# VectorE of layer 0's attention in written order, with row work and routing in parts

## The chip, the cores and the metric

One Trainium2 chip, of which the kernel uses one core. The core has TensorE (PE, matmuls into PSUM banks), VectorE (DVE), ScalarE (ACT), GpSimd (POOL) and SyncE (SP, whose queue issues most DMAs); each works through its own list of instructions in a fixed order, and semaphores make one wait for another. The metric is the device time of one execution in microseconds.

## The reference

Two layers over x of 8 x 512 x 512 (batch, row, feature), float32. Layer 0 is causal attention with 16 heads of 32, then a mixture of 8 experts of which each row uses two; after each a layer norm. Layer 1 (attention with 8 query heads over 2 key heads, then a quantised FFN) is not touched by the change. Layer 0, cut to what matters:

```python
q, k, v = (x @ W.T + b for W, b in ((WQ_w, WQ_b), (WK_w, WK_b), (WV_w, WV_b)))      # in heads
attn = softmax(where(causal, -inf, q @ k.T / sqrt(32)))
x = layernorm(x + (attn @ v) @ WO_w.T + WO_b)
probs = softmax(x @ gate_weight.T + x @ (2.0 * gate_lora_B @ gate_lora_A).T)
routing_weights, selected = top_k(probs, 2)          # and divided by their sum
x = layernorm(x + sum over the two of weight * expert(x))
```

## The kernel before

Attention of layer 0 (`attention0`, lines 1353 to 1823) runs over 8 batches b. A batch has 4 groups g of 4 heads, and a group has 3 units u, which are the key tiles (0), (1, 3) and (2) of the causal triangle. One pass of the innermost loop is called the slot (g,u) here: 12 slots a batch. A slot issues, in the order of its text:

- `scores` (L1603): matmuls of q and k into the one room `sc` (four PSUM banks), for the third unit of batches 1 to 6 preceded by `deltas` (adapters of the experts); ScalarE's exp to `p`, GpSimd's `affine_select` of the causal diagonal, and beside them other GpSimd work: `watch_inverses` (adds r_inv to g_total, L1129), the addition of the bias row to x (L1638; for batch 0 in one instruction, L1641), and the merging of adapters into expert weights (L874);
- `todo[g, u]`: work planned for this slot, mostly matmuls with the addition that takes their result out of the bank;
- `waiting` (`product`, L1647): p times values of the slot before into `av`, and VectorE's sums of p of the units over the keys (`total`, L1665, for the second and third unit);
- `late[g, u]`: more planned work;
- in the second unit `summing` (`normalise`, L1668) of the group before: matmuls `rs` of `total` with ones; ScalarE's copy, Ln and Exp; VectorE's two steps that refine the inverse (L80, L81), and the product with av into aoT (L1679).

`plan` (L1692) says what lies in which slot. Query, key and value matrices of batches 1 to 7 are made by a scheme with seven products instead of eight (`queries_and_keys`, `values`; their matmuls `ps_1of7` to `ps_7of7` in the order 1, 6, 2, 5, 3, 7, 4). The sums of blocks that feed them are `seven_of_weights` (once, L812) and `seven_of_rows` (per batch, on xT, L825). `project` (L1528) multiplies aoT by wo, adds it to x, and after the fourth row tile calls `env.layernorm` (L217 to L225: statistics, then GpSimd's rstd, then four normed row tiles, each stored to DRAM). `blocks` (L1556) transposes the normed rows in 32 x 32 blocks on VectorE and sends them through DRAM to get x transposed; `score` (L1575) makes router logits of it, `choose` (L1587, L537) the two experts of each row in some 26 small VectorE instructions, `dispatch` (L1590) the rank of each row in its expert in 13, `one_hot` and `enter` (L1595, L1600) put rows into the table of tiles.

Results of matmuls other than sc, av and (before) ps_r lie in two banks that alternate, `mm`. A matmul into one of them waits until the content from two calls back has been read.

What sets the order: `in_order` (L70) fixes TensorE's list to the order of the text. VectorE, ScalarE, GpSimd and SP are not fixed in this part: a planner puts their instructions in an order by when it reckons them ready, at build time, and on the chip that order stands. `issue_after` (`behind_return`, L1550) makes instructions follow a given one on the same queue.

## Time and profile before

| | us |
|---|---|
| median of 3 runs | 2144.84 (2137.78 to 2147.74) |
| profiled execution | 2130.51, its span 2128.7 |
| granted TensorE clock | 0.996 |
| attention of layer 0, first scores to the last slot | 14.25 to 716.5 |
| one batch in the middle (batch 4) | 369.89 to 456.45 |
| TensorE busy in 197 to 628 (431 us, batches 2 to 6) | 397.91 |
| VectorE busy there | 325.21 |
| GpSimd busy there | 189.59 |

Start times below are microseconds from the start of the span. A timeline line is: start, length, engine, line of the kernel, operation, names of what it writes and reads, shapes, how many were merged into the line, and in brackets the idle time of the engine before it with what ended it. In the list of waits, `PE rs L1672 <- DVE qk L1472` reads: TensorE's matmul into rs waited for VectorE's instruction of line 1472. Seven-product matmuls have line 67, as all matmuls that go through the helper `matmul_by_columns`.

### The profile page before, as it was taken

The numbers are of one execution on the slowest core, as the hardware profiler recorded it, in microseconds if no ns is written. First come the engines' busy times: TensorE is split into PE (matmuls) and PEld (weight loads), VectorE is DVE, ScalarE is ACT, GpSimd is POOL, SyncE is SP. The second block draws the span as 40 slices with busy tenths as digits, with TensorE's granted clock in tenths as the row PEclk, the third lists the DMA queues.
The fourth block names the chain that finished last, engine by engine and source line by source line (L and its number), as shares of the span: only waits on it lengthen the run. The fifth ranks groups of instructions, "written<-read, shape, count | busy, mean of one in ns | idle before, by whom it ended". The sixth has DMA issues, their size and how long they took to land. (4 is left out here: it accounts for less than half of the span.)

```text
span 2128.7 us, 40459 instructions
## 1 busy us (share of the span) xinstructions
PE 2049.1 (96%) x17122; PEld 1117.1 (52%) x17122; DVE 1314.0 (62%) x2155; ACT 638.9 (30%) x930; POOL 517.3 (24%) x509
## 2 busy tenths in 40 slices
PE   8888999999997999999999999999999999999998
PEld 2334444444443677775433333333334888888886
DVE  4657876877867733224236888888857644555443
ACT  2334334343443211111133333333332232222222
POOL 1343534444443311132033312322201000000000
PEclk9999999999999999999999999999999999999999
DMA  6014425235154467887631322232201311111000
GB/s 204 2 57 124 141 80 144 88 103 155 61 176 169 169 169 222 248 243 214 188 113 51 114 75 72 98 119 75 65 1 47 102 60 60 60 60 60 20 20 22
DMA packets 193071, 226.29 MB, mean 106 GB/s; under 512 B 73818, under 2 KB 139610, under 8 KB 189298
## 3 DMA queue, kind: packets, MB, share of 16 engines
q1 hardware_dynamic: 180240, 185.44, 27.8%
q0 software_dynamic: 10560, 34.61, 5.6%
q10 hardware_dynamic: 2082, 3.56, 0.6%
q8 instruction: 138, 2.26, 0.4%
q14 instruction: 51, 0.42, 0.1%
HBM read 138.88 MB, written 84.69 MB: 105 GB/s over the span
## 5 line engine op out<-in xcount | busy, mean ns | idle before, releaser
L1618 ACT ACTIVATE p<-sc 128x2048 f32<-128x2048 f32 (+1 forms) x96 | 152.4, 1587 | 194.6 <-PE sc L67 194.6
L1628 POOL TENSOR_SCALAR_AFFINE_SELECT p<-p 128x512 f32<-128x512 f32 x128 | 98.4, 780 | 383.6 <-ACT p L1618 379.9
L1281 DVE SCALAR_TENSOR_TENSOR hT<-ps_u,vec,sg 128x512 f32<-128x512 f32 x88 | 65.5, 745 | 189.8 <-PE ps_u L1276 189.6
L1292 PE MATMUL ps_f<-ffn_w,h_half 128*128 128x512 f32 x664 | 167.6, 393 | 2.8 <-DVE h_half L1287 2.0
L1009 PE MATMUL ps_gu<-xrT,experts 128*128 128x256 f32 x736 | 166.7, 379 | 0.0
L1009 PEld LDWEIGHTS ps_gu<-xrT,experts 128*128 128x128 f32 x736 | 139.3, 190 | 35.9 <-issue 19.3
L1129 POOL TENSOR_TENSOR g_total<-g_total,r_inv 128x512 f32<-128x512 f32 x64 | 87.7, 1370 | 289.7 <-DVE r_inv L2035 270.6
L2005 ACT ACTIVATE p<-sc 128x1024 f32<-128x1024 f32 x128 | 124.2, 1022 | 100.0 <-PE sc L67 96.5
L1665 DVE TENSOR_TENSOR p<-p 128x1536 f32<-128x1536 f32 (+2 forms) x96 | 147.2, 1533 | 7.9 <-POOL p L1628 2.9
L2035 DVE RECIPROCAL r_inv<-r_inv 128x512 f32<-128x512 f32 x32 | 107.1, 3347 | 71.5 <-ACT r_inv L1126 71.5
L1292 PEld LDWEIGHTS ps_f<-ffn_w,h_half 128*128 128x128 f32 x664 | 122.9, 188 | 34.4 <-DVE h_half L1287 7.4
L1276 PE MATMUL ps_g<-x_high,ffn_w 128*128 128x512 f32 x352 | 137.2, 390 | 0.0
L1276 PE MATMUL ps_g<-x_low,ffn_w 128*128 128x512 f32 x352 | 137.0, 389 | 0.0
L1276 PE MATMUL ps_u<-x_low,ffn_w 128*128 128x512 f32 x352 | 136.9, 389 | 0.0
L1276 PE MATMUL ps_u<-x_high,ffn_w 128*128 128x512 f32 x352 | 136.9, 389 | 0.0
L67 PE MATMUL sc<-qT,kT 64*64 64x512 f32 x1024 | 124.7, 602 | 1.2 <-ACT qT L1899 0.9
L2024 PE MATMUL av<-p,v 128*64 128x512 f32 x512 | 120.8, 593 | 0.0
L1279 ACT ACTIVATE sg<-ps_g,vec 128x512 f32<-128x512 f32 x88 | 60.6, 688 | 195.4 <-PE ps_g L1276 195.4
L67 PE MATMUL ps_o<-attn_out,aoT 128*64 128x512 f32 x512 | 116.4, 598 | 0.0
L67 PE MATMUL ps_q<-hT,attn_qkv 128*64 128x512 f32 (+1 forms) x504 | 116.2, 596 | 0.0
L1126 ACT ACTIVATE r_inv<-rs 128x512 f32<-128x512 f32 x64 | 38.2, 597 | 254.6 <-PE rs L1672 109.2
L219 POOL TENSOR_SCALAR rstd<-mv 128x4 f32<-128x4 f32 x15 | 3.9, 260 | 452.9 <-DVE mv L218 452.9
(317 smaller groups left out, 3584.3 us busy)
## 6 DMA issues: line engine op xcount, KB each, us to landing
results<-y SPq DMA_DIRECT2D x68, 256.0 KB, 2.7
pair<-xrT SPq DMA_DIRECT2D x30, 512.0 KB, 3.1
xrT<-pair SPq DMA_DIRECT2D x120, 128.0 KB, 3.8
turned<-turned SPq DMA_DIRECT2D x56, 256.0 KB, 4.0
merged<-merged SPq DMA_DIRECT2D x48, 256.0 KB, 2.8
experts<-merged SPq DMA_DIRECT2D x8, 1536.0 KB, 8.3
x<-in_x SPq DMA_DIRECT2D x8, 1024.0 KB, 8.7
merged<-in_gate_up SPq DMA_DIRECT2D x32, 256.0 KB, 3.0
```

The source lines that it names most:

```text
L67: nc.tensor.matmul(out[m], lhsT=lhsT[:, m], rhs=rhs, start=start, stop=stop)
L1009: nc.tensor.matmul(ps[:, j, :], lhsT=w, rhs=xT[:, c, :], start=c == 0, stop=c == ND - 1)
L1129: self.nc.gpsimd.tensor_tensor(self.total, self.total, r_inv, ALU.add)
L1276: nc.tensor.matmul(ps, lhsT=w[:, ts(dc, P)], rhs=x[:, dc, :], start=(dc, i) == (0, 0), stop=(dc, i) == (ND - 1, 1))
L1281: nc.vector.scalar_tensor_tensor(hT, u, vec[:, V_SU + c : V_SU + c + 1], sg, ALU.mult, ALU.mult)
L1292: self.nc.tensor.matmul(os[t], lhsT=h[:, ts(t, P)], rhs=self.weights(2 * NHID + c), start=(c, i) == (0, 0), stop=(c, i) == (NHID - 1, 1))
L1618: nc.scalar.activation(p, sc[:, :, :width], AF.Exp, scale=scale)
L1628: select = nc.gpsimd.affine_select(out=first, in_=first, pattern=[[0, 4], [1, P]], compare_op=ALU.is_ge, fill=0.0, base=0, channel_multipl ...
L1665: nc.vector.tensor_tensor(total[:, :, P * kt :], total[:, :, P * kt :], p[:, :, at : at + w], ALU.add)
L2005: nc.scalar.activation(p, sc, AF.Exp, scale=scale)
L2024: nc.tensor.matmul(st["av"][HD * j : HD * (j + 1), :], lhsT=st["v"][:, kt, HD * j : HD * (j + 1)], rhs=p[:, j, :], start=kt == 0, stop=kt ...
L2035: nc.vector.reciprocal(r_inv, r_inv)
```

## The change

VectorE's list is fixed to the order of the text too, from the first query up to the slot (2,1) of the last batch; and the text is put in a new order.

- A slot now ends with `summed` (the sums of p of the slot before, split off `product`) and a third list, `after`.
- `normalise` ends with ScalarE's rough inverse; VectorE's part (`finish`) comes in the third unit of the slot after, behind `todo`.
- `project` takes its statistics with each row tile; `norm_rows` norms and stores two row tiles in `after` of (2,0) and two in (2,1). `blocks` is split over `after` of (2,2) and (3,0); the next x is loaded behind it.
- The router's logits move from (3,2) to (0,0) of the next batch, the matmul and first two steps of the choice to (0,1), its other 24 instructions (`pick`) to `after` of (0,1), the dispatch to `after` of (0,2), `one_hot` in halves to (1,0) and (1,1). ps_r lies in an mm bank and no longer in an av bank.
- Sums of blocks of weights and rows are split and spread; `spread` is made a slot ahead of its matmuls.
- In the last batch the products of the second pair of heads are spread from (0,0) to (2,2), and experts 1 and 2 are loaded a group later. `watch_inverses` moves from the third unit to the first.

```diff
-        nc.scalar.activation(tmp, tmp, AF.Exp)
+        nc.scalar.activation(tmp, tmp, AF.Exp)
+        return lambda: self.pick(here, pr, tmp, top, second, red, total, bc)
...
+            if t == 0:
+                stats[:] = env.small.tile([P, NT, 6], F32, name="stats"), env.small.tile([P, NT, 2], F32, name="mv")
+            nc.vector.bn_stats(out=stats[0][:, t, :], in_=xs[b][:, t, :])
+            nc.vector.bn_aggr(out=stats[1][:, t, :], in_=stats[0][:, t, :])
...
+        def norm_rows(b, *tiles):
+            for t in tiles:
+                x = xs[b][:, t, :]
+                nc.vector.tensor_scalar(x, x, stats[1][:, t, 0:1], stats[2][:, t : t + 1], ALU.subtract, ALU.mult)
+                nc.sync.dma_start(out=router.rows[router.row_at(b, t) :][:P], in_=x)
...
-            if u == 2 and inverses:
+            if u == 0 and inverses:
...
+        def sum_up(u, p, acc):
+            total, at = acc[0], 0
+            for kt in UNITS[u] if u else ():
                 w = S - P * kt
-                if u:
-                    nc.vector.tensor_tensor(total[:, :, P * kt :], total[:, :, P * kt :], p[:, :, at : at + w], ALU.add)
+                nc.vector.tensor_tensor(total[:, :, P * kt :], total[:, :, P * kt :], p[:, :, at : at + w], ALU.add)
...
-                inverse(nc, r_inv, rs, work.tile([P, S], F32, tag="r_inv", name="r_rough", bufs=2))
+                rough = rough_inverse(nc, rs, work.tile([P, S], F32, tag="r_inv", name="r_rough", bufs=2))
+            def finish():
+                if (b, g) != (NB - 1, ND - 1):
+                    inverse(nc, r_inv, rough)
+                normed[0] = nc.vector.tensor_tensor(aoTs[b][:, g, :], av, r_inv, ALU.mult)
...
                     (0, 0): [lambda: value(0, 0), lambda: value(0, 1)],
-                    (0, 1): [lambda: value(0, 3), lambda: query(0, 1)],
-                    (0, 2): [lambda: value(0, 2), lambda: key(0, 1), lambda: pair_of_heads(0, 1)],
-                    (1, 0): [lambda: router.merge_lora(mm([P, ND, E], "ps_wr")), lambda: query(0, 2), lambda: key(0, 2), x_sums],
-                    (1, 1): [lambda: query(0, 3), v_sums],
-                    (1, 2): [lambda: key(0, 3), q_sums, out_of_bias],
-                    (2, 0): [k_sums],
+                    (0, 1): [lambda: value(0, 3), lambda: query(0, 1), lambda: v_sums(False)],
+                    (0, 2): [lambda: value(0, 2), lambda: key(0, 1), lambda: pair_of_heads(0, 1), lambda: q_sums(False)],
+                    (1, 0): [lambda: router.merge_lora(mm([P, ND, E], "ps_wr")), lambda: query(0, 2), lambda: key(0, 2),
+                             lambda: v_sums(True), lambda: k_sums(False)],
+                    (1, 1): [lambda: query(0, 3), lambda: x_sums(False), spread_bias],
+                    (1, 2): [lambda: key(0, 3), out_of_bias, lambda: q_sums(True), lambda: x_sums(True)],
+                    (2, 0): [lambda: k_sums(True)],
...
-                    todo[2, 0].append(x_sums)
+                    late[1, 2].append(lambda: x_sums(False))
+                    late[2, 0].append(lambda: x_sums(True))
...
+                after[3, 0].append(lambda: load_next_x(b + 1))
             if b > 1:
-                todo[0, 0].append(lambda: choose(b - 2, mm=aside))
-                late[0, 2].append(lambda: dispatch(b - 2))
+                late[0, 0].append(lambda: score(b - 2))
+                todo[0, 1].append(lambda: picks.append(choose(b - 2)))
+                after[0, 1].append(lambda: picks[0]())
+                (late if last else after)[0, 2].append(lambda: dispatch(b - 2))
+                for places, slot in zip(((0, 1), (2, 3)), (((0, 2), (1, 0)) if last else ((1, 0), (1, 1)))):
+                    after[slot].append(lambda places=places: rows.append(one_hot(b - 2, places)))
+                todo[1, 2].append(lambda: enter(rows[-1]))
...
+                for tiles_of, slot in zip(((0, 1), (2, 3)), ((1, 1), (1, 2)) if last else ((2, 0), (2, 1))):
+                    after[slot].append(lambda tiles_of=tiles_of: norm_rows(pb, *tiles_of))
                 if by_dma:
-                    todo[2, 1].append(lambda: blocks(pb))
-                    late[3, 2].append(lambda: score(pb))
+                    after[2, 2].append(lambda: blocks(pb, 0, 1))
+                    after[3, 0].insert(0, lambda: blocks(pb, 2, 3))
...
-        order.enter_context(in_order(tc))
+        order.enter_context(in_order(tc, mybir.EngineType.DVE))
...
-                    for e in ((0,), (), (1, 2), (3, 4, 7))[g]:
+                    for e in ((0,), (), (), (1, 2, 3, 4, 7))[g]:
                         experts.load(e)
                 acc = []
                 for u in range(len(UNITS)):
                     p = scores(b, g, u)
                     for thunk in todo[g, u]:
                         thunk()
+                    if u == 2 and finish is not None:
+                        finish()
                     if waiting is not None:
                         waiting()
                     for thunk in late[g, u]:
                         thunk()
                     if u == 1 and summing is not None:
-                        summing()
+                        finish = summing()
+                    if summed is not None:
+                        summed()
+                    for thunk in after[g, u]:
+                        thunk()
                     waiting = lambda b=b, g=g, u=u, p=p, acc=acc: product(b, g, u, p, acc)
+                    summed = lambda u=u, p=p, acc=acc: sum_up(u, p, acc)
+                    if (b, g, u) == (NB - 1, 2, 1):
+                        order.close()
+                        order.enter_context(in_order(tc))
```

## The prediction

> **What bounds the kernel now.** First the page: TensorE (PE) is busy for 96% of the span, VectorE (DVE) for 62%.
>
> ```profile
> span 2128.7 us, 40459 instructions
> PE 2049.1 (96%) x17122; PEld 1117.1 (52%) x17122; DVE 1314.0 (62%) x2155; ACT 638.9 (30%) x930; POOL 517.3 (24%) x509
> ```
>
> So an edit of VectorE's order pays or costs only where TensorE stands still for VectorE. The list of waits, filtered to TensorE and to batches 2 to 6 (197 to 628 us), shows where; the columns are total, times, longest:
>
> ```profile
> PE rs L1672 <- DVE qk L1472: 10.5, 10, 1.1
> PE ps_4of L67 <- DVE experts L1472: 6.9, 5, 1.4
> PE ps_3of L67 <- DVE qk L1472: 4.7, 5, 0.9
> PE ps_5of L67 <- DVE qk L1472: 4.7, 5, 0.9
> PE ps_rank L67 <- DVE qk L1506: 3.2, 5, 0.7
> PE rs L1672 <- DVE x L1532: 3.0, 4, 0.9
> ```
>
> Every line is a matmul that wants one of the two mm banks while VectorE has not yet added the bank's last content into SBUF. The timeline of batch 4 shows why one of them is late: the 24 small instructions of the choice run from 374.65 to 381.2, the addition of ps_2of is behind them, and rs waits for its bank.
>
> ```profile
> 374.65 0.19 DVE L554 TENSOR_REDUCE red<-tmp 128x4 f32<-128x32 f32 x1 [1.01 <-ACT tmp L553]
> ...
> 378.49 1.27 DVE L581 TENSOR_TENSOR earlier<-earlier,both 128x8 f32<-128x8 f32 x3
> 379.80 1.22 DVE L582 TENSOR_TENSOR r_carry<-earlier,both 128x8 f32<-128x8 f32 x1
> 381.05 0.17 DVE L579 COPY earlier<-r_carry 128x8 f32<-128x8 f32 x1
> 381.13 0.68 DVE L1472 TENSOR_TENSOR qk<-ps_2of,qk 128x512 f32<-128x512 f32 x1
> ```
>
> ```profile
> 381.87 1.07 PE L1672 MATMUL rs<-p,ones 128*32 128x512 f32 x8 [1.02 <-DVE qk L1472]
> 384.93 1.93 PE L67 MATMUL ps_3of<-experts 128*32 128x256 f32 x32 [0.95 <-DVE qk L1472]
> 390.10 0.24 PE L67 MATMUL ps_rank<-both,r_before 128*32 128x32 f32 x5 [0.64 <-DVE qk L1506]
> ```
>
> One more reading decides much below: VectorE's and GpSimd's (POOL's) instructions hold each other up. In batch 0 the sums of p take 6.95 us instead of 2.5, for as long as GpSimd's 6.02 us addition lasts, and TensorE loses 4.54:
>
> ```profile
> 72.83 6.95 DVE L1665 TENSOR_TENSOR p<-p 128x1536 f32<-128x1536 f32 x2 [0.17 <-PE av L1657]
> ```
>
> ```profile
> 73.21 6.02 POOL L1641 TENSOR_TENSOR x<-x,row 128x2048 f32<-128x2048 f32 x1
> ```
>
> ```profile
> 80.44 3.39 PE L67 MATMUL ps_5of<-experts 128*32 128x256 f32 x32 [4.54 <-DVE qk L1472]
> ```
>
> **TensorE's steps.** Start to start in batch 4: scores 1.05 (third unit 0.57, its deltas 0.49), a product of seven 1.75, av 0.87 (third unit 0.48), rs 0.98, a projection 3.46, logits 0.97, table 0.87, ps_r 0.29, rank 0.26. With 12 scores, 4 deltas, 21 products of seven, 12 av, 4 rs, 4 projections and one each of the rest that is 78.4 us; the batch lasts from 369.89 to 456.45, 86.56. So 8.1 us a batch are stalls: 4.2 in A, slots (0,1) to (1,1); 2.3 in B, (2,1) and (2,2); 1.5 in C, (3,2). The change leaves TensorE's work as it is (logits move by a slot, ps_r goes from an av bank to an mm bank, which puts one more turn between the two banks). What it can win is these stalls; what it can lose is new ones. I therefore walk VectorE's written order against TensorE's steps over the three stretches where VectorE has most to do. VectorE starts 0.26 after a product's last step (0.18 until its end, 0.08 lag).
>
> **A, the choice and the dispatch.** In written order the choice comes after the fifth product's addition, and everything behind it waits. From the start of rs: TensorE needs rs 0.98, slot (0,2) 5.69, scores 1.05, product four 1.75, so the first projection could start at 9.47. It needs the bank of rank, which VectorE has read only after: lag and addition 0.91; the choice; product three's two additions 0.88; the deferred inverse and its product 2.1 (three of 0.69 to 0.73); product seven's two 1.25; sums of p 2.45; five instructions of the dispatch 0.9. That is 8.5 and the choice. The choice took 4.7 in the last batch (695.14 to 699.87, four of its instructions slipped between others, so 5.1 one by one) and 6.0 in batch 4 (6.6 less the addition inside it). The new place is worse: it runs over the first 5 us of (0,2), where GpSimd has its select (3.0 to 4.0 us after the slot's start) and then two merges of 1.75 each. I take 6.8: 5.1, and one of these waits in full. A stalls 8.5 + 6.8 - 9.47 = 5.8, and 0.6 more for one select (0.64) before the sums of p in (1,0): 6.5. Bounds: 4.1 with no collision; 9.2 with the select (0.96), both merges and the later select in full. Against 4.2: +2.3 (-0.1 to +5.0).
>
> **B, row work and sums of rows.** From the third projection's last step: TensorE needs table, av, scores, projection, product one, av, scores, product six, av and product two, 13.9, to rs. VectorE: lag 0.26, addition and statistics 1.6, table 1.4, inverse 2.1, two sums of rows 1.72 (0.86 each), sums of p 2.45, the last projection 1.6, two sums of rows 1.72, sums of p 1.7 (1.22 to 2.18 in the timeline), two rows normed 0.93 (1.92 for four), product six's addition 0.65: 16.1. Stall 2.2. Three of GpSimd's instructions of 1.2 to 1.3 fall here (g_total, select, x plus row); I count one, 3.4 in all. Bounds 1.7, and 5.0 when rstd (1.3 on GpSimd) comes behind another. Against 2.3: +1.1 (-0.6 to +2.7). For norm_rows, which waits for rstd, product six's addition is behind it, and rs waits for that.
>
> **C, blocks.** From the fifth product in (2,2): TensorE 7.6 to product four; VectorE lag and addition 0.94, inverse 2.1, product three 0.9, sums of p 2.45, two transposes 1.24, product seven 1.25: 8.9. Stall 1.3, with a part of a merge 1.7 (1.2 to 3.0). Against 1.5: +0.2. In (3,2), where C's stall is now, product three's addition comes ahead of the inverse and the stall goes.
>
> Small ones: in (0,0) and (3,1) VectorE now idles for a product with a sum of p ready behind it; the trace of before has the reverse, so I bound it by 0 and 1.0 a batch and take 0.5. Steady: 2.3 + 1.1 + 0.2 + 0.5 = +4.1 a batch, times five +20.
>
> **The other batches.** Batch 0 (waits 4.5, 1.6, 1.1): the sums of p no longer meet GpSimd's long addition ahead of product five, spread is made a slot early, weights' sums are spread over five slots of 8 to 9 us with 3 to 6 us of VectorE work: -6.5 (0 to -7.2). Batch 1 (110.05 to 196.84, 86.79 less steps 77.0: 9.8 idle) has no choice and no table: A goes, B 2.9, C 1.7: -5 (-7 to 0). The last batch idles 10.7 by its rows. Its three postponed products (5.25) now lie in (1,2) to (2,2), from where on TensorE waits 6.0 for others, and can win 3.5; but A has less TensorE work to hide the choice: pick and dispatch stall rank 2.3, the first projection 0.8, the second 3.3, and 1.5 of collisions, 7.8 against 4.6. Net 0 (-6 to +6). Loads of experts 1 to 4 start after (2,2), which ended at 688.4, and no more in (0,2) and (1,0); five overlapping loads took 6 to 12 us each, and the first is wanted at 712.22: nothing.
>
> Queues: SP gets two stores a slot in place of four at once, and the turned blocks go out some 17 us later (from 423.8 to the end of (3,0), 438.7, and the stalls). The next x is issued behind their return; it landed at 442.73, its first reader is GpSimd's addition at about 466, so 23 us of cover shrink to 6. Priced at nothing while this lasts. The sums of rows waited up to 2.0 for xT on VectorE (landed at 399.46); written, they come after 410, so that wait goes, and it covered no wait of TensorE. On GpSimd g_total moves from the third unit to the first, behind the select.
>
> Sum: 20 - 6.5 - 5 + 0 = +8.5, and 0.8 each for the same idling of VectorE in batches 0, 1 and 7: +11. The profiled execution took 2130.51, so 2141.5. The median of the runs is 14.3 above it; the same step from 2144.84 gives 2156. A measurement of this kernel can tell about 0.5%, 10.7 us, from no change.
>
> [...]
>
> **The rivals.** *It pays:* GpSimd's work falls between, the choice costs 5.1, and A, B and C stall 4.2, 2.0 and 1.3, as much as before less 0.5. Then -2.5, batches 0 and 1 -11.5, the last -2: -16, 2129. For it: the 33 us of waits above, all for banks. Against it: VectorE has 13.5 us on end in (0,2) and (1,0) (5.1, 0.9, 2.1, 1.25, 2.45 and 1.7 for the dispatch), and TensorE's steps there are 12.4. It decides if the choice stays under 5.5. *Even:* half the collisions, +1.5 a batch, 7.5 against 9: 2143. *Late x:* if the return and x take over 6 us longer than before, GpSimd's addition in (0,1) holds the next select, av waits, some 5 us in six batches: +30 on top of 11, 2186.
>
> **How the numbers follow.** Forecast 0.48 (its own range 2149 to 2168; 0.10 of it lies within 0.5%), it pays 0.28, even 0.16, late x 0.08. Faster 0.28, same 0.26, slower 0.46. The low end 2125 is "it pays" with the lower bounds of batches 0 and 1; the high end 2182 leaves most of late x out.
>
> **What would show it.** Right: in batch 4 a wait of rank, of the fourth product and of the first projection, together 5 to 8 us, all for VectorE; rs in (2,1) waits 2 to 3; no 4.5 us wait in batch 0; merges beside the choice's last additions. Wrong: a batch under 86 us, or an av that waits for GpSimd's select.

## The result, and the profile after

The changed kernel takes 2174.6 us (median of 4 runs, 2171.9 to 2180.06), the kernel before 2141.32 beside it: a ratio of 1.0155, 95% interval 1.0119 to 1.0191. It is slower, as forecast, but by 33 us instead of 11. The profiled execution took 2176.42. One execution of the last run of the experiments, 3011.0 us at a granted clock of 0.654 where the others have 0.993 to 0.996, is left out of its figures.

The page of the changed kernel, its span and the busy times:

```profile
span 2174.7 us, 40447 instructions
PE 2075.6 (95%) x17122; PEld 1128.7 (52%) x17122; DVE 1323.6 (61%) x2155; ACT 640.3 (29%) x930; POOL 507.4 (23%) x509
```

The same 17122 matmuls keep TensorE busy for 26.5 us longer (2049.1 before). So of the 46.0 us between the two spans only 19.5 are waiting. The rest is matmuls that ran slower. By stage, each from the first scores of one batch to the first scores of the next (us):

| | before | after | difference | predicted |
|---|---|---|---|---|
| batch 0 | 95.8 | 88.6 | -7.2 | -6.5 |
| batch 1 | 86.8 | 85.2 | -1.6 | -5 |
| batches 2 to 6 | 431.5 | 473.3 | +41.8 | +20 |
| last batch | 88.2 | 96.9 | +8.7 | 0 |
| what comes after | 1412.2 | 1416.1 | +3.9 | not named |

Batches 2 to 6 hold nearly all of it. The rows by windows say what kind of time it is; first the kernel before, then the changed one. Columns: window, its length, busy time (and instructions) of TensorE, weight loads, VectorE, ScalarE and GpSimd, then TensorE's granted clock, the share of the DMA engines, GB/s.

```profile
196.80:628.40 431.60, 398.51 (x6852) 188.56 (x6848) 325.54 (x646) 170.54 (x235) 189.59 (x170) 1.00 0.37 113
```

```profile
188.20:661.70 473.50, 421.83 (x6848) 199.15 (x6844) 337.34 (x645) 171.37 (x235) 181.35 (x170) 0.94 0.34 103
```

Idle time of TensorE rose from 33.1 to 51.7, by 18.6; its busy time by 23.3, with the granted clock down from 1.00 to 0.94.

The list of TensorE's waits in the changed kernel, batches 2 to 6 (total, times, longest):

```profile
PE ps_4of L67 <- DVE qk L1481: 23.0, 10, 2.7
PE ps_rank L67 <- DVE qk L1515: 13.2, 5, 3.3
PE ps_6of L67 <- DVE x L1481: 10.4, 5, 2.1
PE ps_o L67 <- DVE mine L605: 2.8, 5, 0.6
PE ps_1of L67 <- DVE qk L1515: 1.5, 5, 0.3
PE rs L1712 <- DVE qk L1481: 0.8, 1, 0.8
```

Before, the longest wait of these batches was 1.4, spread over six places. Now there are three stretches with waits of 1.9 to 3.3, and all are still for banks that VectorE has not read: A is rank (13.2), five of the ten fourth products (1.87 each) and the first projection (2.8); B is product six; C is the other five fourth products (2.72 each).

A in batch 4, VectorE's timeline. The choice runs from 390.98 to 398.85:

```profile
390.98 0.18 DVE L563 TENSOR_REDUCE red<-tmp 128x4 f32<-128x32 f32 x1
...
392.18 1.00 DVE L569 TENSOR_TENSOR tmp<-pr,top 128x32 f32<-128x32 f32 x1
...
395.78 0.93 DVE L581 TENSOR_TENSOR r_weights<-top,total 128x4 f32<-128x4 f32 x1
396.64 0.15 DVE L582 TENSOR_TENSOR r_weights<-second,total 128x4 f32<-128x4 f32 x1
396.71 1.25 DVE L586 TENSOR_TENSOR both<-r_hots 128x32 f32<-128x32 f32 x1
...
398.77 0.87 DVE L1515 SCALAR_TENSOR_TENSOR qk<-ps_3of,steps,qk 128x256 f32<-128x256 f32 x2
```

Two products of the same size take 0.93 and 0.15. GpSimd has two merges there, one until 396.70 and the next from 396.66 to 397.92. The longer product ends with the first merge, at 396.71; the shorter one falls where the two meet; and the step of 1.25 behind it ends with the second merge, at 397.96. The merges in GpSimd's timeline:

```profile
395.43 2.49 POOL L883 TENSOR_TENSOR merged<-merged,scaled 128x512 f32<-128x512 f32 x2 [0.68 <-ACT scaled L874]
```

Behind the choice the addition that frees rank's bank waits, and TensorE's timeline shows the price:

```profile
399.79 0.24 PE L67 MATMUL ps_rank<-both,r_before 128*32 128x32 f32 x5 [3.09 <-DVE qk L1515]
...
403.03 3.64 PE L67 MATMUL ps_4of<-experts 128*32 128x256 f32 x32 [1.87 <-DVE qk L1481]
407.23 4.08 PE L67 MATMUL ps_o<-experts,aoT 128*32 128x512 f32 x32 [0.56 <-DVE mine L605]
```

Read the lengths as well as the waits. The fourth product takes 3.64, where a product of seven takes 1.93 at the full clock; the first projection takes 4.08 instead of 3.64. The same stretch by windows, and beside it the row that shows why (the third column from the right is the granted clock):

```profile
400.00:402.00 2.00, 1.16 (x31) 0.24 (x17) 1.93 (x4) 0.73 (x1) 0.00 (x0) 0.84 0.77 170
402.00:404.00 2.00, 0.97 (x12) 0.60 (x16) 2.00 (x3) 1.15 (x1) 0.78 (x1) 0.50 0.90 307
404.00:406.00 2.00, 2.00 (x25) 0.99 (x20) 1.86 (x5) 0.00 (x0) 2.00 (x2) 0.50 0.76 285
406.00:408.00 2.00, 1.45 (x12) 0.23 (x8) 1.83 (x9) 0.00 (x0) 0.72 (x1) 0.50 0.05 18
```

Behind the 3.09 us wait the clock stands at one half for 6.83 us, from 401.36. The records of the clock show 17 such stretches in the attention of layer 0, of 3.41 or 6.83 us, 81.9 us in all; before there were three, 13.7 us in all. In batches 1 to 6 they follow all five stalls of A, four of the six of B and five of the six of C; the last batch has three. So 14 of these 17 stalls are paid for twice, once as waiting and once by slow matmuls behind it.

B in batch 4, VectorE, and TensorE's product six:

```profile
425.43 0.69 DVE L84 SCALAR_TENSOR_TENSOR r_inv<-r_inv,r_rough 128x512 f32<-128x512 f32 x1
426.15 0.69 DVE L85 SCALAR_TENSOR_TENSOR r_inv<-r_inv,r_rough 128x512 f32<-128x512 f32 x1
429.12 0.69 DVE L1723 TENSOR_TENSOR aoT<-av,r_inv 128x512 f32<-128x512 f32 x1 [2.29 <-PE ps_o L67]
```

```profile
434.35 2.59 PE L67 MATMUL ps_6of<-experts 128*32 128x256 f32 x32 [2.09 <-DVE x L1481]
```

VectorE is not short of time here: it stands still for 2.29 us. aoT is one buffer; the product of group 0 writes into it, and the last projection of the rows before still reads it. Everything written behind that product, with the addition that product six wants, comes 2.29 later.

C in batch 4, VectorE, GpSimd and TensorE:

```profile
445.01 1.78 DVE L84 SCALAR_TENSOR_TENSOR r_inv<-r_inv,r_rough 128x512 f32<-128x512 f32 x1
446.83 1.64 DVE L85 SCALAR_TENSOR_TENSOR r_inv<-r_inv,r_rough 128x512 f32<-128x512 f32 x1
...
452.61 1.29 DVE L129 STREAM_TRANSPOSE x1T<-x 128x512 f32<-128x512 f32 x2
```

```profile
444.96 2.96 POOL L883 TENSOR_TENSOR merged<-merged,scaled 128x512 f32<-128x512 f32 x2
```

```profile
455.22 2.96 PE L67 MATMUL ps_4of<-experts 128*32 128x256 f32 x32 [2.72 <-DVE qk L1481]
```

The two steps of the inverse take 1.78 and 1.64 instead of 0.69 each while GpSimd merges; with the two transposes of 1.29 behind them, product four waits 2.72 and then runs at half clock.

### The profile page after: what moved, and what is told of

Same layout as the page of the kernel before. It is cut to its first block, busy times and chain, and to the rows that moved or that the text cites. A ratio compares the mean times of both kernels' runs of the same rounds, so it can differ in the third digit from the quotient of the medians.

```text
span 2174.7 us, 40447 instructions
## 1 busy us (share of the span) xinstructions
PE 2075.6 (95%) x17122; PEld 1128.7 (52%) x17122; DVE 1323.6 (61%) x2155; ACT 640.3 (29%) x930; POOL 507.4 (23%) x509
## 5 line engine op out<-in xcount | busy, mean ns | idle before, releaser
L1138 POOL TENSOR_TENSOR g_total<-g_total,r_inv 128x512 f32<-128x512 f32 x64 | 92.2, 1440 | 277.1 <-DVE r_inv L2104 270.0
L1705 DVE TENSOR_TENSOR p<-p 128x1536 f32<-128x1536 f32 (+2 forms) x96 | 123.2, 1284 | 5.8 <-PE av L1696 2.1
L67 PE MATMUL ps_o<-experts,aoT 128*32 128x512 f32 x896 | 106.0, 616 | 5.9 <-DVE qk L1481 3.1
```

The costliest lines, as they stand in the source:

```text
L67: nc.tensor.matmul(out[m], lhsT=lhsT[:, m], rhs=rhs, start=start, stop=stop)
L1138: self.nc.gpsimd.tensor_tensor(self.total, self.total, r_inv, ALU.add)
L1705: nc.vector.tensor_tensor(total[:, :, P * kt :], total[:, :, P * kt :], p[:, :, at : at + w], ALU.add)
```

## The experiments

The theory after this reading: the written order makes three separate stalls a batch (A by the choice beside GpSimd's merges, B by the single buffer of aoT, C by the inverse beside merges and the transposes), and most of these stalls also halve the clock behind them. The rivals: VectorE's work in these units is simply too much, so that a stall removed in one place comes back in another; or the text (row work in parts) costs it, and not the order.

Results of all runs; batches 2 to 6, the last batch, and the time at half clock in layer 0's attention are from each run's profiled execution. A ratio is to executions of the kernel before that ran beside that run, with medians of 2139.57 to 2141.75. By the ratios the gains over the changed kernel differ from those of the medians that the text gives: 26 us for text only, 18 for stalls filled, 17 for group 0, 33 for no merges, 16 for the choice, 6 for the turns.

| | median, us | ratio to before (95%) | batches 2-6 | their idle | last batch | half clock |
|---|---|---|---|---|---|---|
| before | 2141.3 | 1 | 431.5 | 33.1 | 88.2 | 13.7 |
| changed | 2174.6 | 1.0155 (1.0119-1.0191) | 473.3 | 51.7 | 96.9 | 81.9 |
| text only | 2149.23 | 1.0035 (1.0019-1.0051) | 452.8 | 46.1 | 89.0 | 41.0 |
| stalls filled | 2155.15 | 1.0072 (1.0049-1.0095) | 459.9 | 19.0 | 94.2 | 17.1 |
| group 0 finished later | 2153.74 | 1.0077 (1.0049-1.0105) | 457.3 | 43.6 | 96.7 | 54.6 |
| no merges | 2138.66 | 1.0000 (0.9983-1.0017) | 443.4 | 36.6 | 93.2 | 37.5 |
| choice in parts | 2156.89 | 1.0080 (1.0055-1.0105) | 454.2 | 43.4 | 96.2 | 37.5 |
| turns later | 2170.0 | 1.0125 (1.0098-1.0152) | 467.4 | 49.7 | 102.0 | 71.7 |
| four moves together | 2128.35 | 0.9939 (0.9921-0.9958) | 427.8 | 27.4 | 101.3 | 20.5 |
| and last batch planned | 2132.56 | 0.9958 (0.9943-0.9973) | 431.4 | 27.5 | 104.2 | 30.7 |
| four moves, batch 6 as changed | 2127.46 | 0.9940 (0.9923-0.9957) | 430.4 | 28.0 | 97.3 | 20.5 |
| last products back | 2170.65 | 1.0142 (1.0124-1.0160) | 468.1 | 50.1 | 96.4 | 68.3 |
| both of these | 2127.53 | 0.9938 (0.9923-0.9952) | 433.9 | 29.7 | 97.8 | 30.7 |
| rows normed early in the last batch | 2128.35 | 0.9929 (0.9901-0.9957) | 431.1 | 28.6 | 93.8 | 17.1 |

**Text only.** VectorE is left to the planner, with the changed text:

```diff
-        order.enter_context(in_order(tc, mybir.EngineType.DVE))
+        order.enter_context(in_order(tc))
```

> The changed kernel with VectorE's list left to the planner and all else of the change kept. Theory (the written order makes the loss: the choice, the inverse and the blocks stand ahead of additions that TensorE needs, and a planner would pull these additions ahead): the time falls back to 2130 to 2150 us, the waits of rank and of the fourth product fall from 13.2 and 27.1 us in layer 0 to under 8 together. Rival (the rearranged text makes the loss, because the planner can't move the inverse's product ahead of a projection either and the logits and the dispatch come later whatever the order): 2165 to 2180 us.

It took 2149.23: 25 us of the 33 belong to the written order. The time is the theory's, the waits are not: rank and the fourth product were to wait under 8 together, and rank alone waits 26.3. The text costs the rest, and the waits in its batches 2 to 6 say where: the choice now lies before rank's bank for the planner too, and is still going on when rank is due.

```profile
PE ps_rank L67 <- DVE qk L1515: 26.3, 5, 5.3
PE ps_4of L67 <- DVE experts L1481: 6.9, 5, 1.4
```

One wait of 5.3 a batch stands in place of A's three; the others are those of the kernel before, or smaller. Batch 0 took 94.5 here, so its gain is the order's doing too.

**Stalls filled.** Matmuls whose result nobody reads are put into the four places where TensorE waits, 9 a batch:

```diff
+        def warm(n):
+            room = p_sc.tile([P, 4, S], F32, tag="sc", name="warm")
+            for i in range(n):
+                nc.tensor.matmul(room[:, i, :], lhsT=wo[:, 0, :P], rhs=wo[:, 1, :], start=True, stop=True)
...
+            if 0 < b < NB - 1:
+                if b > 1:
+                    after[0, 2].insert(0, lambda: warm(2))
+                    after[0, 2].append(lambda: warm(2))
+                after[2, 0].append(lambda: warm(2))
+                late[3, 0].insert(0, lambda: warm(3))
```

> The changed kernel with matmuls that nobody reads in TensorE's stalls of batches 1 to 6 (two of 512 columns before rank, two behind it, two before the scores of (2,1), three before the fourth product in (3,0)). Theory (over half of the loss is the granted clock, which is 0.5 for 3.4 or 6.8 us after a stall: 82 us of half clock in layer 0 against 14 before): half clock falls under 20 us, TensorE's own steps get back to 78.4 us a batch, and the time falls by 15 to 25 us although work is added. Rival (the loss is the idle time alone, the longer matmuls are only a way of counting it): 2175 to 2185 us, no faster.

More work, and 19 us faster. This is the plainest evidence that the clock is a cost of its own. A pair of these products (four records) takes 1.98, so nine take 8.9 a batch and 44.6 in batches 2 to 6; yet TensorE's busy time there rose by only 19.2 over the changed kernel. The other 25, gone with the half clock, are what it had cost, close to the 23.3 by which busy time had risen. The row of these batches, with the granted clock at 1.00, and the products beside rank's shorter wait:

```profile
186.70:646.70 460.00, 440.99 (x6936) 202.81 (x6932) 337.85 (x645) 171.53 (x235) 174.15 (x170) 1.00 0.35 106
```

```profile
387.81 1.98 PE L1741 MATMUL warm<-experts 128*128 128x512 f32 x4
390.98 0.24 PE L67 MATMUL ps_rank<-both,r_before 128*32 128x32 f32 x5 [1.18 <-DVE qk L1515]
```

**Group 0 finished later.** The inverse and the product into aoT of group 0 are moved one unit on, from (1,2) to (2,0), in batches 1 to 6; GpSimd's `watch_inverses` for it follows to (2,1):

```diff
-            if u == 0 and inverses:
+            if (u == 0 or (g, u) == (2, 1)) and inverses:
...
-                    if u == 2 and finish is not None:
+                    later = 0 < b < NB - 1 and ((g, u) == (1, 2) or (g, u) == (2, 0))
+                    if finish is not None and ((u == 2) != later):
                         finish()
```

> The changed kernel with the deferred inverse and its product of the first group moved from (1,2) to (2,0), behind the last projection. Theory (stall B is not VectorE's sum of work: aoT has one buffer, so this product waits 2.3 us for the last projection, and the sums and the addition stand behind it in the list): the 2.1 us wait of the sixth product goes in all six batches, with the half clock behind it 3 to 3.5 us a batch, 18 to 21 us in all. Rival (the prediction's: the sum of the work ahead of rs sets the stall): the same work stays ahead of rs, the wait moves from the sixth product to rs, and the time changes by less than 5 us.

It gained 21 us by the medians, 17 by the ratios. VectorE's work between the projections and the sums of rows is the same; only the wait for the buffer is gone, and with it B's stall: product six starts without a wait and takes 1.93, and the aoT product comes without idle time.

```profile
424.30 1.93 PE L67 MATMUL ps_6of<-experts 128*32 128x256 f32 x32
```

```profile
424.54 0.69 DVE L1723 TENSOR_TENSOR aoT<-av,r_inv 128x512 f32<-128x512 f32 x1
```

What remains of B is 0.94 at rs. That refutes the prediction's account of B, which made it the sum of VectorE's work.

**No merges.** GpSimd's 48 additions that merge adapters into expert weights are left out, so the stored weights of the experts lack their adapters:

```diff
-        return {0: load, 1 + i: lambda: nc.gpsimd.tensor_tensor(w[0], w[0], scaled, ALU.add),
-                2 + i: lambda: nc.sync.dma_start(out=self.merged[:, e : e + 2, f], in_=w[0])}
+        return {0: load, 2 + i: lambda: nc.sync.dma_start(out=self.merged[:, e : e + 2, f], in_=w[0])}
```

> The changed kernel without GpSimd's 48 additions that merge adapters into expert weights (the experts then lack their adapters for the parts that this stage merges). Theory (the choice is slow because GpSimd's instructions hold it up): the choice takes 5.0 to 5.6 us instead of 7.7, the wait of rank falls from 2.3 to 3.3 us to about 1, the inverse in (2,2) falls from 4.1 to 2.2 us and the fourth product's wait in (3,0) from 2.7 to about 1; 15 to 25 us faster. Rival (the choice's 24 dependent instructions are long by themselves): the waits stay within 0.5 us, under 8 us faster.

36 us, more than expected. The choice takes 4.84 in each of the batches 2 to 6; in the changed kernel it takes 6.91, 8.10, 7.87, 7.19 and 7.07. In batch 4 it runs here from 373.90, and nothing in it is stretched but one product (0.38):

```profile
377.31 0.38 DVE L581 TENSOR_TENSOR r_weights<-top,total 128x4 f32<-128x4 f32 x1
377.60 0.15 DVE L582 TENSOR_TENSOR r_weights<-second,total 128x4 f32<-128x4 f32 x1
377.67 0.18 DVE L586 TENSOR_TENSOR both<-r_hots 128x32 f32<-128x32 f32 x1
```

Rank does not wait for 0.25 us in any of the five batches, and C's wait falls from 2.72 to 0.94; B's 2.09 stays. A is not gone: the fourth product still waits 1.5 to 1.9, and the first projection, 0.6 in the changed kernel, 0.9 to 2.3, since the inverse, the sums of p and the dispatch are still ahead of what frees their banks. In batches 2 to 6 idle time falls by 15.1 and busy time by 14.8. So GpSimd's merges, though GpSimd is busy for only 23% of the span, cost the changed kernel 33 to 36 us. The waits of A, 5.1 a batch in the changed kernel, are still 3.8 here: that part does not need the merges. The kernel before has the same merges, and what they cost there no run shows; so it stays open how much of the 33 to 36 belongs to the written order.

**Choice in parts.** The 24 instructions of the choice are cut into three pieces (by `yield` in `pick`, not shown) with other additions between them; dispatch and `one_hot` come one unit later (batches 2 to 6):

```diff
-                after[0, 1].append(lambda: picks[0]())
-                (late if last else after)[0, 2].append(lambda: dispatch(b - 2))
+                    todo[0, 1].append(lambda: next(picks[0]))
+                    after[0, 1].append(lambda: next(picks[0]))
+                    after[0, 2].append(lambda: next(picks[0]))
+                    after[1, 0].append(lambda: dispatch(b - 2))
...
-(((0, 2), (1, 0)) if last else ((1, 0), (1, 1)))
+(((0, 2), (1, 0)) if last else ((1, 1), (1, 1)))
```

> The choice's second half in three parts with TensorE's waiting work between them, and the dispatch, rows and ones that follow it one unit later, in batches 2 to 6; everything else as changed. Theory (stalls of 2 us and more cost twice, once as waiting and once as TensorE at half clock): the 5.6 us that the rank product, the fourth product and the first projection wait per batch fall under 1.5, the 6.8 us of half clock after them goes (some 3 us of work), so 5 to 7 us a batch and 25 to 35 us in all: 2140 to 2150. Rival (the time is VectorE's sum of work in these units and a moved piece is late elsewhere): as much waiting appears in the two following units, 2165 to 2175.

18 us, less than the 25 to 35 expected. A's half clock is gone (no such stretch in (0,1) to (1,1) of any of these batches), but two waits are new, as the rival had it: rank waits up to 1.5 in its new place, and the table up to 1.1 for the `one_hot` that now lies right ahead of it. The two wait 2.3 a batch together, where under 1.5 was expected.

```profile
PE ps_rank L67 <- DVE qk L1484: 6.3, 5, 1.5
PE ps_table L67 <- DVE one_hot L632: 5.4, 5, 1.1
```

Behind rank's wait of 1.48 in batch 4 the next projection takes 3.64, its length at the full clock. B and C are as in the changed kernel.

**Turns later.** The 32 x 32 turns move to the end of (3,0) and into (3,1), with the next load of x:

```diff
-                    after[2, 2].append(lambda: blocks(pb, 0, 1))
-                    after[3, 0].insert(0, lambda: blocks(pb, 2, 3))
+                    after[3, 0].append(lambda: blocks(pb, 0, 1))
+                    late[3, 1].insert(0, lambda: blocks(pb, 2, 3))
...
-                after[3, 0].append(lambda: load_next_x(b + 1))
+                (late[3, 1] if by_dma else after[3, 0]).insert(0, lambda: load_next_x(b + 1))
```

> The first pair of 32x32 turns to behind product seven's additions in the first unit of group 3, the second pair and the next rows of x to the unit after it; everything else as changed. Theory: the fourth product's wait there falls from 2.7 to about 1.4, which is under what sets TensorE to half clock, and 3.4 us of half clock (1.7 us of work) goes: 2 to 3 us in each of six batches, 2156 to 2164. Rival (x is loaded too late): the next batch's addition of x on GpSimd waits for it and the values' sums behind it, av waits, and the time is 2180 to 2200.

2170.0, 4.6 under the changed kernel where 11 to 19 were expected. The mechanism held: C's wait falls from 2.72 to 1.5 in each batch and the half clock behind it is gone; batches 1 to 6 gain 8.5. They gain no more because the half clock in A grew, from 34.1 to 41.0 us in batches 2 to 6, with waits of rank up to 4.6; why rank waits longer the runs do not show. And the last batch takes 5.1 longer, its first router product now waiting for the turned rows:

```profile
PE ps_logits L536 <- DMA x1T<-turned: 5.4, 1, 5.4
```

The rival named the right cause, a transfer that is late, but another transfer.

**Four moves together.** Group 0 later, choice in parts, turns later, and the rows normed one unit later (with the second pair of sums of rows in the unit after):

```diff
-                for tiles_of, slot in zip(((0, 1), (2, 3)), ((1, 1), (1, 2)) if last else ((2, 0), (2, 1))):
+                for tiles_of, slot in zip(((0, 1), (2, 3)), ((1, 1), (1, 2)) if last else ((2, 1), (3, 0))):
...
-                    late[2, 0].append(lambda: x_sums(True))
+                    after[2, 1].append(lambda: x_sums(True))
```

> The inverse and product of group 0 one unit later, the choice in parts, the turns later, and the rows normed one unit later, all in the changed kernel. Theory: the three stalls are separate, so their gains add: a steady batch of 95.5 falls to 82 to 85, and with the last batch as changed the time is 2105 to 2130, below the kernel before. Rival (the work of VectorE moved out of one stall lands in the next): a batch of 88 to 91, 2140 to 2155.

2128.35, faster than both kernels; than the one before by 0.6%, with the interval clear of 1. Batches 2 to 6 take 427.8, 85.6 each, just over the theory's 82 to 85, and there is no half clock in them at all. The gains add: alone, group 0, the choice and the turns won 16.0, 19.1 and 5.9 in these batches, 41.0 in sum, and the four moves won 45.5. The fourth, the rows normed later, was not run alone. The longest wait in batches 2 to 6 is 1.5:

```profile
PE ps_4of L67 <- DVE qk L1484: 7.2, 5, 1.5
PE ps_table L67 <- DVE one_hot L632: 5.5, 5, 1.1
PE ps_rank L67 <- DVE qk L1484: 5.2, 5, 1.2
```

VectorE is busy for 353.7 us in these batches, more than the 337.3 of the changed kernel, and TensorE idles about half as long. The amount of VectorE's work did not set the time, as the first rival had it.

**The last batch.** Five runs tried to win back its 8.7 us, and none did so in the time of the whole kernel. First VectorE is left to the planner from the start of the last batch on the kernel of the four moves:

```diff
-                    if (b, g, u) == (NB - 1, 2, 1):
+                    if (b, g, u) == (NB - 2, 3, 2):
                         order.close()
                         order.enter_context(in_order(tc))
```

> The one before it, and VectorE's order left to the planner from the start of the last batch on, not from the middle of its third group. Theory: the last batch took 96.9 in written order and 89.0 with the planner's order, so 6 to 10 us under the one before it. Rival (the last batch is bound by what it has to do, in any order): within 2 us of the one before it.

A miss: 4.2 over the kernel of the four moves in the median, with overlapping intervals, and a last batch of 104.2; rank waited 9.1 for the choice there. With the text only the planner's last batch had taken 89.0, so its order does not carry over from one text to the next.

Then two more edits, and both of them together. The turns, the norming and the load of x of batch 6 are put back to the change's places (the diff has the turns alone):

```diff
-                    after[3, 0].append(lambda: blocks(pb, 0, 1))
-                    late[3, 1].insert(0, lambda: blocks(pb, 2, 3))
+                    if b == NB - 2:
+                        after[2, 2].append(lambda: blocks(pb, 0, 1))
+                        after[3, 0].insert(0, lambda: blocks(pb, 2, 3))
+                    else:
+                        after[3, 0].append(lambda: blocks(pb, 0, 1))
+                        late[3, 1].insert(0, lambda: blocks(pb, 2, 3))
```

> The kernel with all four moves, but in batch 6 the turns of the last rows that go by DMA, the next rows of x and the norming stay where the change had them, so that the turned rows are back before the last batch starts. Theory (the 5.4 us that the last batch's first logits product waits for the turned rows, and half of the 6.8 us at half clock behind it, are the price of the late turns, and of nothing else): 2128.35 less 5 to 9, that is 2119 to 2124. Rival (the late transfer only lays bare that the last batch is bound by VectorE): within 2 us of 2128.

The 5.4 us wait went and the last batch is 4.0 shorter, but C's wait of 2.7 and its half clock are back in batch 6, which goes from 85.5 to 89.4. The time is the same, where 5 to 9 less was expected. The other edit, on the changed kernel, brings the last batch's three postponed products back into the places of every other batch:

```diff
-                        (todo, 0, 0), (todo, 0, 1), (todo, 0, 2), (todo, 1, 0), (todo, 1, 2), (todo, 2, 1), (todo, 2, 2)) if last else (
                         (todo, 0, 0), (late, 0, 0), (todo, 0, 1), (late, 0, 1), (todo, 0, 2), (late, 0, 2), (todo, 1, 0))):
```

> The changed kernel with the last batch's three postponed products of queries and keys back in the places of every other batch. Theory (the last batch lost 8.7 because 5.25 us of TensorE's work was taken from beside the choice, in the stretch where the rank product and the projections wait 2.5 and 2.4): these waits and the half clock behind them shrink, 5 to 9 us, 2165 to 2170. Rival (VectorE's own chain from the projections to the rows normed sets that stretch, and the products only fill later waits): the wait for the rows in the third group grows by as much, 2172 to 2180.

The last batch takes 96.4 instead of 96.9: the projection waits 0.7 in place of 2.4, but the fourth product 1.1, rank 3.9 in place of 2.5, and the turn 5.3 in place of 4.8. Its ratio of 1.0142 overlaps the changed kernel's. Taking them back wins nothing: the waits move, and the postponed products are not the cause of the loss.

Both edits on the four moves:

> The first and the second of these edits together, on the kernel with all four moves. If the theory holds for both: 2112 to 2119. If the products in the last batch gain nothing: as the first, 2119 to 2124.

They gave 2127.53, the same again, and neither of the two expectations came. The last run looks at the longest single wait of the last batch. VectorE and TensorE in the changed kernel:

```profile
708.00 1.00 DVE L1559 TENSOR_SCALAR x<-x,mv,rstd 128x512 f32<-128x512 f32 x2 [1.48 <-POOL rstd L1553]
...
716.03 1.94 DVE L1559 TENSOR_SCALAR x<-x,mv,rstd 128x512 f32<-128x512 f32 x2
```

```profile
717.57 1.78 PE L1608 MATMUL ps_x1T<-ident,x 128*128 128x128 f32 x6 [4.83 <-DVE x L1559]
```

The second pair of rows is normed 8 us after the first, behind product three's addition, the table, the inverse and the sums of p. The run norms it right behind the first:

```diff
-((1, 1), (1, 2)) if last else
+((1, 1), (1, 1)) if last else
```

> The kernel with the four moves and batch 6 as changed, and in the last batch the second pair of rows normed right behind the first pair, where the change put it behind product three's addition, the table, the inverse and the sums of p. Theory (the 4.8 us that the last batch's turn waits for those rows, and the half clock behind it, are a price of that place in the written order, not of VectorE's work): the wait falls under 1, 5 to 8 us, 2119 to 2123. Rival (the work put behind the rows is waited for instead, by the next product of the queries and keys or by the sums of rows): within 2 us of 2127.5.

The wait is gone and the last batch falls by 3.5, to 93.8, though the scores of (2,2) now wait 2.4 for ScalarE. The time of the kernel did not follow: 2128.35 against 2127.46. In the profiled execution what comes after layer 0's attention took 1419.6 instead of 1414.5, with one wait of 2.9 for a ScalarE result and a half clock behind it that the kernel it is compared with did not have. The run with the last products back, which lacks this edit, has the same wait (2.84), the half clock and the 1419.6 as well, so they can come without it. Why the median shows no gain stays open.

## Why the prediction was right and wrong

The direction was right, and so was the mechanism it stood on: VectorE's additions out of the banks queue behind work that the text puts ahead of them. Idle time in batches 2 to 6 was to rise by 20 and rose by 18.6, but that is partly luck: a batch waited 1.4 less than said in A, 1.1 less in B and 1.3 more in C, the small term of 0.5 did not come, and the 8.1 us of stalls before are 6.6 us of idle time in the trace. The time lay inside the range, but above the forecast's own range of 2149 to 2168, in the part that the range had for late x, and late x did not come: that too is luck.

The step that failed is one sentence in "TensorE's steps": "The change leaves TensorE's work as it is". In number of matmuls it does; in time it added 23.3 us in batches 2 to 6, since the same steps took longer at half clock (a product in A 3.64 in place of 1.93). 78.4 us of steps a batch is no constant: it was read in batch 4 of the kernel before, where the granted clock is 1.00, and in batches 2 to 6 of the changed kernel the clock is 0.94. The prediction had shown the evidence itself: the line at 80.44 of the kernel before has a wait of 4.54 and a product of 3.39 us behind it, where such a record is 1.93 elsewhere; the clock stands at one half there for 3.41 us, from 80.03. It read the wait and not the length. With the clock, +20 becomes about +43, and +11 about +34. Between the profiled executions 45.9 were measured; of the 12 that are left most is the last batch (8.7), what comes after (3.9) and batch 1 (3.4 over its term), less the 2.4 counted for idling in three batches, which does not show.

Term by term:

- **A** was right in kind and somewhat large. The choice was taken as 6.8 and took 6.9 to 8.1; "it pays" was to decide under 5.5. The three waits came to 5.1 a batch against 6.5 predicted (5.5 in batch 4, inside the 5 to 8 named as its sign). That GpSimd stretches the choice is shown by the run without merges, where it takes 4.84 and rank no longer waits; but 3.8 of the 5.1 stay there, so most of A's waiting does not come from the merges.
- **B** was too large (2.1 and a wait of 0.8 once, 2.25 a batch, against 3.4) and wrong in cause. Its sign, a wait of 2 to 3 at rs in (2,1), did not come; product six waited. It was laid to 16.1 us of VectorE's work against 13.9 of TensorE's. VectorE in fact stood still for 2.29 for the buffer of aoT. VectorE's list of waits in the kernel before had held the same wait, which the prediction did not look up:

```profile
DVE aoT L1679 <- PE ps_o L67: 9.5, 5, 1.9
```

There it cost TensorE less, with other work of VectorE put ahead of it; in the written order it stands ahead of everything. The kernel of the four moves does the same work and product six does not wait.
- **C** was undersized: 3.0 (2.72 and 0.29) against 1.7. A part of one merge was allowed for, and both steps of the inverse were stretched, by 2.0 in all.
- **Batch 0**: -7.2 against -6.5, its long wait gone as described.
- **Batch 1**: -1.6 against -5. Its idle time fell from 7.3 to 6.6 only. B's 2.9 came (2.09 and 0.80); C waited 2.72 in place of 1.7, the first projection 0.71 that was not in the sum, and half clock behind C brought busy time to 78.6 against steps of 77.0. The 9.8 "idle" from which the prediction started held half clock too (busy 79.5).
- **The last batch**: +8.7 against 0, by 4.1 of idle time and 4.7 of busy time, with half clock for 17.1 us in place of 6.8. Its choice took 9.5 between GpSimd's merges and selects, av waited 2.6 for a select (the prediction's own sign of being wrong, seen in this batch alone), and the turn waited 4.83 for the second pair of normed rows, 1.63 before, where the postponed products were to win 3.5. Undoing only the last of these, in a run, made the batch shorter by more than 1 us (3.5).
- **Late x** did not come. The load was issued at 469.35 in batch 4; its first reader, GpSimd's addition at 486.13, followed the select before it directly.
- **From the profiled execution to the median** 14.3 us were added, the distance before. The changed kernel's profiled execution was 1.8 above its median, so of 45.9 us between the profiled executions 33.3 remain between the medians, and a miss of 35 us there is one of 22 here. The profiled execution of the kernel before was faster than any other on record of it.

The upper bound of A, 9.2, did not come: A waited 5.1 a batch. What the runs show of the collisions behind that bound: two small instructions of the choice in batch 4 end with the instruction of GpSimd beside them (396.71 and 396.70, 397.96 and 397.92), and the choice takes 2.1 to 3.3 us more in the changed kernel than the 4.84 without the merges.

## What to carry to other kernels

When a change of one engine's order moves stalls about, add up not only the idle time of the engine that bounds the kernel but also the length of its first instructions behind each stall; a table of granted clock by windows shows at once whether a stall costs twice. In batches 2 to 6 of the four moves, where no wait is longer than 1.5 us, there was no half clock; in the changed kernel a wait of 2.1 had 3.41 us of it behind it in four of six batches. So cutting a long run of small instructions into pieces paid here (18 us by the medians, 16 by the ratios), even though new waits of up to 1.5 appeared. In a list in written order, look for the instruction that waits for a buffer, not only for the sum of the work: moving one such group by a unit was worth 17 to 21 us, and four such moves took the kernel below the one it started from.

## What the runs showed of the hardware that was not expected

The starts of half clock lie on a grid. In the profiled execution of the changed kernel the 17 of layer 0's attention (169.25, 210.21, 244.35 and so on, to 715.39) lie at whole multiples of 3.413 us from each other, and so do the three of the kernel before (80.03, 144.88 and 691.02). Cutting batches 1 to 6 of the 14 profiled executions along that grid and adding up TensorE's idle time in each window that lies wholly in them gives:

| clock in the window | idle in it, us | windows | followed by half clock |
|---|---|---|---|
| full | under 0.8 | 1780 | 0 |
| full | 0.8 to 1.5 | 185 | 1 |
| full | 1.5 to 2.0 | 43 | 3 |
| full | 2.0 and more | 64 | 62 |
| half | under 0.8 | 68 | 2 |
| half | 0.8 and more | 21 | 21 |

So half clock followed 62 of the 64 full-clock windows with 2.0 us of idle time and more, and 4 of the 2008 with less; behind a window at half clock it went on in all 21 cases with 0.8 us and more, and in 2 of the 68 with less. In the kernel before and the changed one alone these are 14 of 14, 1 of 280, 5 of 5 and none of 15. What makes the clock do so, no run shows.

A in batch 4 is such a case: the window up to 401.36 holds the last 1.84 of rank's wait and the first 0.20 of the fourth product's, 2.04 in all, and half clock follows; the next holds the other 1.67 of the fourth product's wait, and half clock goes on for a second window. In B the same wait of 2.09 was followed by half clock in four of the six batches 1 to 6; in the other two it straddles two windows (1.33 and 0.76, 0.19 and 1.90), and none followed. So equal waits cost differently by where they lay on the grid. Whether that makes a part of the difference between executions of one kernel was not tested; on record is that time goes with the granted clock, with a mean of 2133.9 us in two executions of the kernel before at 0.996 and of 2144.0 in three at 0.990.
